# The second row's value sum over the experts: its last terms added by TensorE with the identity, in a new hand-written order of the whole program

## The chip, the cores and the metric

The kernel runs on one core of one Trainium2 chip. The metric is the device time of one execution in microseconds (us); the time of a kernel is the median of its runs. The granted TensorE clock of the profiled execution is 1.00.

## The reference, cut to what matters

The input x has two rows of 128 tokens and 512 channels, and a context of 2048 tokens stands beside each row. Three layers follow each other, each added to x: a perceiver layer (self-attention, cross-attention over the context, a feed-forward part, three layer norms), an RWKV7 layer whose scan runs over the two rows (so row 1 needs the state of row 0), and a SwitchHead attention over the 128 tokens of each row. The change is in the last one, with H = 8 heads of DH = 64, E = 5 experts and SEL = 2:

```python
q = (x @ Wq).reshape(b, t, h, dh).transpose(0, 2, 1, 3)
k = (x @ Wk).reshape(b, t, h, dh).transpose(0, 2, 1, 3)
gl_v = (x @ Ws).reshape(b, t, h, e)
wv = _topk_mask(gl_v, SEL) * jax.nn.sigmoid(gl_v)
xv = jnp.einsum('btd,edk->btek', x, Wv)
v = jnp.einsum('bthe,btek->bhtk', wv, xv)
scores = jnp.einsum('bhid,bhjd->bhij', q * scale, k)
probs = jax.nn.softmax(scores, axis=-1)
attn = jnp.einsum('bhij,bhjd->bihd', probs, v)
gl_o = (x @ Wd).reshape(b, t, h, e)
mask_o = _topk_mask(gl_o, SEL)
out = jnp.einsum('bthe,bthk,ekd->btd', mask_o, attn, Wo)
```

A head's value is the sum over the five experts of a gate times that expert's value. This sum, `v`, is what the change touches.

## The kernel before, in words

Tokens lie on the 128 partitions. Weights are multiplied in full f32 or, where they were split into a high and a low half (names with `hl_`), in fp32r. The phases are functions: queries, self-attention, cross-attention, feed-forward, `rwkv` and `switch_heads`, each called for row t = 0 and row t = 1. The weights of the later phases are loaded by SP's DMA queue while the earlier phases run.

**Order.** The phases do not run as they are written. `Program` records every engine call in a list, and `emit` issues the calls in the order of the list of numbers `ORDER` (lines 42 to 98), so that work of both rows and of several phases is interleaved by hand. Each engine runs its own instructions in that order and waits where an operand isn't ready. All recorded instructions have line 169 in the profile, the line in `emit`; they are told apart by the names of their tiles. DMA issues on SP are in the list too. Tiles come from pools that rotate: eight PSUM banks (`bank`), twenty row tiles (`row`), sixteen wide tiles (`wide`).

**switch_heads** (lines 1019 to 1150), for one row:

- `xn` is the normed row: its first half by DVE, its second by ACT, once a rinv has come from POOL. PE turns it (xnT).
- PE multiplies xnT with `fcat` (both gates' logits and the experts' values in one matrix of 400 columns, four matmuls), with `fWq` and with `fWk` (16 matmuls of 128x128 each). ACT copies gl, xv, qT and kT out of PSUM.
- DVE makes the gates: gt, eq, eq, gt and ahead count for each expert how many logits stand ahead of it, sel keeps those with fewer than two ahead, wv is the value gate.
- The value sum (lines 1058 to 1077): four products wv*xv go into the wide tile `ve`, the fifth into `v`, each 128x512; then three adds on DVE: `ve` 128x1024 (line 1075), `ve` 128x512 (line 1076), `v` 128x512 (line 1077).
- For each half of the heads PE makes the scores kT·qT, DVE reduces their negated maximum `nb`, ACT the exponentials `es`, PE turns them, ACT copies them (`eT`), and PE multiplies `v` with `eT` (v·eT).
- DVE spreads the result over the experts (`me`, two products of 128x1280 in row 0; one and three pieces in row 1) and adds the `me` parts. In row 0 PE turns the sum; in row 1 PE adds and turns it by matmuls with `unit`, an identity matrix in f32. ACT copies `aT`, PE multiplies with `fWo` (per row six matmuls of 128x256), DVE adds the residual (`res`), and SP stores it.

`keep_warm` (line 515) issues dummy matmuls of `unit` with `unit` into a bank that is overwritten later; TAILW holds their numbers in the tail. `matmuls` (line 344) accumulates a list of products in one bank, `project` (line 455) makes products in two halves of 256 columns, `Moments` (line 358) holds the steps of a norm.

In `rwkv`, what the prediction's steps touch stands at the end: `Y` is scaled by the gate `tg` and turned (yT), multiplied with `Wo` (eight matmuls of 128x256), the residual is added (`hh`), normed and turned (hhT), multiplied with `Wf` (eight matmuls); DVE adds the bias (`f`), ACT takes its tanh (`tf`), and after a norm the row `X` is updated, from which `switch_heads` takes `xn`.

Of the kernel before, what the change touches and what calls it, by code (L numbers as in the profile page):

```python
# [16 lines left out]
P = 128  # L17
# [5 lines left out]
HD = 64  # L23
H = C // HD
# [18 lines left out]
8 0 208 1708 1731 1 209+1 3 215+3 233 1732+1 219+2 211 4 2 232 234 21 235 212 236 213+1 20 25 222+3 228+1 237+4 244  # L43
248+1 270 245 242 22 230 271+1 246 23 273+2 247 26 24 276+1 27 278 231 250+9 279+4 260+5 284 266 285+4 267 37 28 31 34
19 38 226 29 292 30 243 318 32 293+1 33 319+2 295 227 35+1 322+4 39 296+5 43 46 44 47 327+2 302 290 48 40 303+2 269
306+2 330 41 268 309+5 45 11 5 42 9 315 331+6 291 338 317 414 339+2 358 344 359 415 316 69 84 70 49 375 343 345 376
342 50+1 416+1 377+1 360 346+1 12 379 57 418 380+1 18 419 348+2 361 351 382 58 423 79 383 420 13 16+1 15 421+1 14
384+2 352+2 74 355 387+2 424 59 362 390 425+2 363+2 356 391 357 392 428 366 395 367 429 393 368 6 60 87 369 430 394
1709 396+3 372+1 370 431 371 61 432 400 434 1710 402 401 1711 435 56 433 404 436 405 403 437+2 408+1 406 410 463 453
411 440 407 454 464 441 465+1 85 455 467 456 443 457 444 458 442 447 89 448 459 468 71 445 469 483 473 460 446 449 75  # L50
474 470 475 450 476 62 66 77 63 477 88 471 478+1 64 480 484+1 481 486+1 86 488 461 521 493+1 489+1 495 522 126 482 462
496+1 523+2 67 491 498+1 65 500 526 501 68 527+2 502 472 72 492 503+1 530+1 90 505+1 532 507+3 533 511+3 92 515+1 534
94 73 82 535+4 517 549 540 588 76 541+1 589 543 78 544 590 10 518 591+2 80 519 83 550+1 575 552 95 553 545 112 594 576
595 554 104 81 96 546 97 547 555 596 577 597 556 578 557+3 598 98 548 599 727 579+1 520 99 93 91 728 561 107+1 105 121
581+1 562 583 563+5 584 569+4 585 729 106 600 100 129 127 574 586+1 601+1 730+5 603+1 128 618 736 609+2 737+1 740 131
741+2 172 612 766 744+1 1734 767 753 101 746+1 754+1 748 756+1 102 758+1 749 607 605 608 768+5 606 613 137 122 103 760
614 761 623 615 142 641 624 774 625 750+1 642 130 626 109 643 762 644 775+1 374 123 763 173 152 124 616 627 764 777
113 125 628+8 645 739 646 136 659 637 660+1 638 662 639 134 765 114 778 132 617 752 640 647+4 663 145 110 53 664 779
652+1 780 133 781 111 782 654+3 789 783 796 785 135 787 658 55 665+2 677 668 678 669 786 619 784 788 143 679 670+1 790
680+1 672+4 682 138 140 683+2 791 620 792+1 801+2 819 804 820 115 621 174 622 794 837 821 838 686 688 822 839 687 840  # L60
689 147 805 54 807 692 795 146 141 139 693 808 806 809 797+1 116 810 690 811+1 696 813+1 697 815 823 144 824 816+2 694
691 148 698+3 118+1 702+1 855+1 117 704 695 120 705+2 841 149 842 857+1 150+1 52 412 160+1 413 708 710+1 709 712+2 187
171 859 188 825+11 843+3 715 178 153 451 847+7 189 179 860 720+1 716+1 861+2 722+1 718+1 864 904 916 905 866 180 867
865 906+1 917 908 868 874 162 875 909 876 870 877 871 724 928 198 725 869 163+1 799 878 918 910+1 154+1 872 879 157
165 452 156 170 158 175 873 913 880+3 800 884+1 726 159 912 914+1 919+2 886 922 888 176 923 887 925 929 889+1 924
930+1 891+1 932+1 193 934 177 197 926 935 927 936 194 937 893 938+1 184 940 894+1 898 896+1 899+2 957 969 958+1 970
941 943 196 942 944+2 951 948 947 960 952 949 953 950 954 961+1 185 955 963+1 971+2 966 974+1 965 967+1 956 976 978
977 169 195 982+3 1010 979 1012 1011 980 986 186 987+1 1013+1 168 989+2 1016 1015 1020 992+1 1017 1067 1028 1075 1089
1069 1090 1018 1093 1099+1 1107 1111 1022 1029 1092 1091 1101 1076 1102 1094 1142 1077 1030 190 902 1021 191 981 1071
1031 903 1068 1070 1078 1032 1095+1 1079 1108 1112 996 994 1026 1073 1110 1141 1024 997 995 192 998 1072 167 999  # L70
1080+2 1004 1001 1000 166 1083 1005 1002 1023 1084 1033 1006 1003 1103 1034 1109 1085 1007 1074 1008 1086 181 205 1139
182 1035+1 183 1009 1097 1219 1088 1221 1218 1220 1222 1025 1037+1 1224 1027 1039 1225 1223 1098 1113 1116+1 1019 1228
1323 1333 1324 1118 1114 1104 1226 1229 1305 1325 1327 1306 1119 1326 1328 1087 1045 1230+1 1105 1279 1281 1280 1282
1334+2 1329 1232 1344 1330 1233 1042 1283+1 1286+2 1234 1345 1041 1106 1115 1289 1285 1290 1235 1043 1291+2 1237 1046
207 1040 1238 1294 1239 1295 1240 1346 1047 1296 1236 1241 1297 1120 1044 1389 1331 1391 1332 1343 1352 1347 1307 1242
1353 199 1243 1143 1354+1 1244+1 1348 1246 1349+1 204 1140 1048 1054 1121 1337 1056 1065 1123 1122 1390 7 1338 1049
1124 1339 1125 1050 1059 1247 1052 1308 1135 1248 1309 1055 1392 1298+1 1127 1144 1310+2 1393 1061 1300 1058 1145
1340+1 1063 1053 1301 1356 1302 1316+1 1146 1342 1062 1064 1051 1060 1318 1148 1129 1133 1057 1351 1066 1126 1303 1253
203 1319 1376 1136 1252 1357 1249 1137 1251 1256 1304 1254 1250 1138 1255 1377 1130 1358 1257 1264 1258 1260 1378 1262
1131+1 1153 1313 1128 1154 1265 1359 1263 1261 1134 1320 1267 1149+2 1147 1394 1259 1395 1271 1155 1274 1152 1379 1156  # L80
1314 1321 1158+1 1315 1157 1371 1161 1360 1396 1160 1397 200 1170+1 1162 1322 1276 1398 1164 1380 1273 1373 1163 1165
1172+1 1272 1166+1 1277 1268 1374 1190 1361 1375 1278 1381 1270 1174 1383 1175 1168 1269 1367 1382 1362 1364 1169 1366
1384 1363 1176 1275 1177 1372 1385 206 1178 1386+2 1179+1 1368 1365 1369 1266 1370 1399+1 1198 1404 1406 1405 1407+1
201 1401+1 1181+2 1186 1184 1187 1191 1185 1192 1188 1193 1189 1194 1199+1 1195 1409 1403 1196 202 1410+1 1197 1201+4
1412 1415 1413+1 1424 1416+1 1425+1 1206+1 1212 1209 1208 1213 1210 1214 1211 1215+2 1473 1472 1427 1418+2 1475+1 1474
1477 1421 1428 1478 1422 1429 1423 1479+1 1487 1481 1488 1482 1430+3 1435 1483 1522 1489 1434 1436+2 1484 1523 1227
1485 1444 1440+1 1439 1450 1505 1442 1451+1 1443 1453 1506+3 1445+1 1486 1447 1496+1 1490+3 1454+1 1458 1524 1498+1
1513 1525 1500+1 1514+1 1502 1511 1516 1526 1517 1503 1518 1494 1510 1448 1512 1449 1459 1456+1 1460 1495 1519+2 1527
1461 1528 1466 1529 1504 1539 1530 1540+1 1463 1462 1467 1464 1468 1465 1469 1542 1470+1 1533 1604+1 1531 1606+1 1610
1608 1559 1609 1560+1 1532 1543 1562 1619 1544 1549 1611 1534 1545 1613 1550 1612 1614+2 1546 1552 1536 1547 1553 1563  # L90
1565 1564 1569 1620 1570 1566 1535 1617 1548 1643 1537 1551 1567 1538 1621+1 1555+1 1554 1638 1637 1639+2 1654 1642
1618 1571 1645 1557 1655 1646+1 1628+1 1558 1648+1 1572+2 1656 1650 1657 1651 1579 1652 1630+1 1575 1623 1632+1 1576+2
1634+1 1624+2 1658 1653 1659 1627 1636 1660+2 1698+3 1671 1568 1644 1664 1667 1665+1 1663 1672+2 1681 1715 1682+1 1716
1582 1580 1583 1581 1587 1688+2 1717 1684 1584 1702+1 1705 1585 1675 1679 1676 1685 1718 1677+1 1712 1691 1588 1692
1686 1589 1668 1706 1704 1586 1590+1 1713 1719 1669 1687 1670 1694 1693 1695+2 1592 1714 1721 1707 1727 1680 1720
1725+1 1722+2 1593 1599+2 1594 1728 1735 1729 1741 1730 1747 1595 1736+1 1596 1738+1 1742+3 1748+2 1740 1751 1597+1
1746 1758 1752 1759 1602 1760+2 1753+2 1603 1756+1
"""
OPT = set("""psc me2 z1d fc2 Wv Wk u2col bfpe z4pe z1pe q2 hhcol q2row d3 both1 both4""".split())

ON_ACT = [set("vsum vc vv bv".split()), set("vsum vc vv bv".split())]
PCR = [{0,1,2},{0,1,2}]
WHOLE = set("Wv1 Wv2 fc2 Wv Wk".split())
VPE = set()
MIX = {"Wq1": 2}
MIXD = set("Ww Wa Wr".split())
Z4D, BFD = {0, 1}, {1}
CUTW = 2
HNORM = "dve"
ACC = set()  # L110
TAILW = (4, 4, 4, 3, 3)
WIDE_W = set("Wq1 Wk1".split())
NDUM, TDUM, HLB, WDB, UNS = 8, 0, 4, 8, 0


class Halves:

# [68 lines left out]
def perceiver_kernel(ctx: ExitStack, tc: tile.TileContext, a: dict, out: bass.AP):  # L186
# [832 lines left out]
    def switch_heads(t):  # L1019
# [91 lines left out]
        for par in range(2):  # L1111
# [11 lines left out]
            if not t:  # L1123
                dve.tensor_add(me[par][:, 0:2], me[par][:, 0:2], me[par][:, 2:4])
# [112 lines left out]
```

## Time and profile before

| what | value |
| --- | --- |
| runs of the kernel before | 221.88, 222.58, 222.99 us; median 222.58 us |
| the profiled execution | 221.38 us |
| its span, first to last instruction | 219.5 us |
| recorded instructions | 3664 |
| DMA | 43.42 MB, mean 198 GB/s |

The profiled execution's time stands 1.9 us above its span and 1.2 us below the median of the runs. Times in the profile count from the start of the span. A line of a timeline gives start, duration, engine, line, operation, output and inputs, shapes and the number of instructions merged in it; in square brackets stands the idle time of the engine before it and what released it. A plain f32 matmul leaves two records in the trace, a transpose or an fp32r matmul one. Recorded durations of neighbouring instructions overlap by a little, so that sums are made from start to start.

### The profile page before, as it was taken

Reading aid. Unit: us, or ns where it says so; the run is one execution under the profiler, and the core shown is the slowest. Engines: PE = TensorE matmul, PEld = TensorE weight load, DVE = VectorE, ACT = ScalarE, POOL = GpSimd, SP = SyncE. Lnnn points to the kernel's source line nnn. Section 1 sums busy time; section 2 is a strip of 40 time slices with the busy share of each in tenths; the row PEclk is TensorE's granted clock in tenths of the full one; section 3 lists DMA queues with packets and bytes.
Section 4 is the critical chain, followed back from the end, with each engine's and each line's share of the span. In section 5 each row is a group of like instructions: output and inputs, shape, how many; then the busy total and the mean of one; then the engine's idle time right before and its main releaser. Section 6 shows DMA issues by size and latency. Waiting matters only on the chain.

```text
span 219.5 us, 3664 instructions
## 1 busy us (share of the span) xinstructions
PE 211.3 (96%) x1228; PEld 178.2 (81%) x1228; DVE 190.0 (87%) x452; ACT 141.2 (64%) x400; POOL 17.6 (8%) x40
## 2 busy tenths in 40 slices
PE   6999999999999999999999999999988999999993
PEld 6999779988787758868788888887765799799892
DVE  4691688999999999988999999999997689999871
ACT  2766578873799899626579599988642524813710
POOL 4200020000000000010120200040302111000000
PEclk9999999999999999999999999999999999999999
DMA  5999999049699894887999999000000000000002
GB/s 181 349 384 378 382 389 361 26 134 362 253 358 392 318 325 157 276 311 263 298 378 401 344 387 355 35 1 0 3 0 0 0 3 1 0 3 0 0 25 73
DMA packets 21897, 43.42 MB, mean 198 GB/s; under 512 B 1283, under 2 KB 2871, under 8 KB 21879
## 3 DMA queue, kind: packets, MB, share of 16 engines
q1 hardware_dynamic: 21879, 43.19, 55.2%
q8 instruction: 10, 0.16, 0.3%
q14 instruction: 8, 0.07, 0.1%
HBM read 42.66 MB, written 0.52 MB: 197 GB/s over the span
## 4 chain that ended last, share of the span: by engine, by line
PE 58%; DVE 23%; issue 11%; POOL 3%; ACT 3%; POOLq 0%; DVEq 0%; ACTq 0%
PE bank L169 58%; DVE ve L169 3%; DVE Y L169 2%; DVE st L169 2%; POOL rinv L169 2%; DVE me L169 2%; DVE nb L169 1%; DVE X L169 1%; DVE v L169 1%; DVE f L169 1%; POOL rs L169 1%; DVE pr L169 1%; DVE gt L169 1%; DVE eq L169 1%; ACT es L169 1%
## 5 line engine op out<-in xcount | busy, mean ns | idle before, releaser
L169 POOL TENSOR_TENSOR rinv<-ve,nhalf 128x1 f32<-128x1 f32 x16 | 10.4, 651 | 146.9 <-DVE ve L169 137.0
L169 DVE TENSOR_TENSOR hl_ctxT<-cT,hl_ctxT 128x1024 fp32r<-128x1024 f32 x16 | 18.9, 1217 | 0.2 <-ACT hl_ctxT L169 0.2
L169 PE MATMUL bank<-hl_ctxT,qkTh 128*128 128x512 f32 x64 | 18.4, 400 | 0.0
L169 ACT CAST hl_ctxT<-cT 128x1024 fp32r<-128x1024 f32 x16 | 16.3, 1052 | 3.3 <-DMA cT<-in_ctxT_dram 3.3
L169 PE MATMUL bank<-hl_ctxN,pTh 128*128 128x512 f32 x48 | 16.2, 410 | 0.0
L169 DVE TENSOR_TENSOR hl_ctxN<-cN,hl_ctxN 128x1024 fp32r<-128x1024 f32 x12 | 14.3, 1215 | 0.0
L169 PEld LDWEIGHTS bank<-hl_ctxT,qkTh 128*128 128x128 f32 x64 | 11.8, 188 | 2.7 <-DVE some L169 0.3
L169 DVE TENSOR_TENSOR hl_Wv<-w_Wv,hl_Wv 128x512 fp32r<-128x512 f32 x12 | 8.0, 684 | 5.2 <-ACT hl_Wv L169 5.2
L169 ACT CAST hl_ctxN<-cN 128x1024 fp32r<-128x1024 f32 x12 | 12.3, 1050 | 0.0
L169 PE MATMUL bank<-unit 128*128 128x128 f32 x58 | 9.3, 315 | 1.7 <-POOL unit masks.py:199 1.7
L169 PEld LDWEIGHTS bank<-unit 128*128 128x128 f32 x58 | 8.8, 229 | 2.0 <-POOL unit masks.py:199 1.7
L169 PEld LDWEIGHTS bank<-hl_ctxN,pTh 128*128 128x128 f32 x48 | 8.9, 188 | 2.0 <-DVE pTl L169 0.2
L169 PE MATMUL bank<-xnT,w_fWq 128*128 128x128 f32 x64 | 10.0, 280 | 0.0
L169 PE MATMUL bank<-hl_ctxT,qkTl 128*128 128x512 f32 x32 | 9.8, 394 | 0.0
L169 PE MATMUL bank<-hl_ctxN,pTl 128*128 128x512 f32 x24 | 9.6, 400 | 0.0
L169 PE MATMUL bank<-xnT,w_fWk 128*128 128x128 f32 x64 | 9.4, 277 | 0.0
L169 PEld LDWEIGHTS bank<-xnT,w_fWq 128*128 128x128 f32 x64 | 8.6, 192 | 0.5
L169 PEld LDWEIGHTS bank<-u2T,w_fc 128*128 128x128 f32 x64 | 7.9, 191 | 1.3 <-ACT u2T L169 0.6
L169 PEld LDWEIGHTS bank<-xnT,w_fWk 128*128 128x128 f32 x64 | 8.3, 192 | 0.6
L169 ACT CAST hl_Wv<-w_Wv 128x512 fp32r<-128x512 f32 x12 | 7.4, 620 | 2.0 <-DMA w_Wv<-in_Wv_dram 1.9
L169 PE MATMUL bank<-u2T,w_fc 128*128 128x128 f32 x64 | 8.2, 277 | 0.3 <-ACT u2T L169 0.3
L169 PE MATMUL bank<-w_Wr,mix 128*128 128x256 f32 x32 | 8.5, 379 | 0.0
(291 smaller groups left out, 607.0 us busy)
## 6 DMA issues: line engine op xcount, KB each, us to landing
cT<-in_ctxT_dram SPq DMA_DIRECT2D x8, 1024.0 KB, 8.2
cN<-in_ctx_dram SPq DMA_DIRECT2D x8, 1024.0 KB, 6.7
spread<-in_spread_dram SPq DMA_DIRECT2D x9, 512.0 KB, 8.4
w_Wv<-in_Wv_dram SPq DMA_DIRECT2D x12, 256.0 KB, 5.4
w_Wk<-in_Wk_dram SPq DMA_DIRECT2D x8, 256.0 KB, 5.0
w_Wq<-in_Wq_dram SPq DMA_DIRECT2D x4, 256.0 KB, 3.7
w_Wk2T<-in_Wk2T_dram SPq DMA_DIRECT2D x4, 256.0 KB, 8.7
w_Wq<-in_Wq_dram SPq DMA_DIRECT2D x1, 1024.0 KB, 11.5
```

The costliest lines, as they stand in the source:

```text
L169: self.tc.keep_in_program_order(op(*args, **kwargs))
```

## The change

In row 1 (`VPH = {1}`), the adds of lines 1076 and 1077 are no longer made by DVE. A new PSUM bank `pv` takes three matmuls of PE with `unit`, moving `v`, `ve[:, 0]` and `ve[:, 1]`, each 128x512 f32, accumulated; a second row tile named `v` takes the result by an ACT copy of 128x512. The 1024-wide add of line 1075 stays on DVE, and so does the whole sum in row 0. The new constant HS0 is 0, with which the lines around `me` do what they did.

```diff
+VPH = {1}
...
+HS0 = 0
...
             dve.tensor_add(ve[:, 0:2, :], ve[:, 0:2, :], ve[:, 2:4, :])
-            dve.tensor_add(ve[:, 0, :], ve[:, 0, :], ve[:, 1, :])
-            dve.tensor_add(v, v, heads(ve[:, 0, :]))
+            if t in VPH:
+                pv = bank([P, H, HD])
+                matmuls(pv.rearrange("p h d -> p (h d)"), [(unit, x) for x in (v.rearrange("p h d -> p (h d)"), ve[:, 0, :], ve[:, 1, :])], True)
+                v = heads(row("v"))
+                act.copy(v, pv)
+            else:
+                dve.tensor_add(ve[:, 0, :], ve[:, 0, :], ve[:, 1, :])
+                dve.tensor_add(v, v, heads(ve[:, 0, :]))
...
-            if not t:
+            if not t and HS0 < 2:
                 dve.tensor_add(me[par][:, 0:2], me[par][:, 0:2], me[par][:, 2:4])
-        if t:
+        if t or HS0:
```

Apart from this, no instruction is added or taken out: PE has three matmuls more, DVE two operations fewer, ACT one more. The extra bank and the extra row tile shift the rotation of the later ones of row 1 by one place. The list `ORDER` is replaced as a whole. On the engines this moves, among others:

| engine | before | after |
| --- | --- | --- |
| SP | w_Ww, ..., fWo, w_Wg, fWk, fWq, w_Wo, w_Wf, fcat | fWk, w_Wo, fWq, w_Ww, w_Wg, w_Wf, fcat, fWo |
| DVE | xn of row 0, then the hh adds of row 1 | hh adds of row 1, then xn of row 0 |
| DVE | gate work of row 0 (gt to wv) and one ve product ahead of xn of row 1 | behind it |
| DVE | me of row 0, among it nb of row 1, then the 1024-wide add of row 1 | nb of row 1 twice and the 1024-wide add, then me of row 0 |
| PE | fcat of row 0 ahead of Wf of row 1 | behind it |
| PE | scores of row 0, first half, ahead of xn's transposes of row 1 | behind them |
| PE | v·eT of row 0 ahead of the scores of row 1 | seven of eight behind them |
| PE | thirteen dummies from 201 us on | nine there, four between Wf of row 0 and the fWk matmuls of row 0 |
| PE | the last fWo matmul of row 0 among the unit·me matmuls | behind them; one fWo matmul of row 1 among them |

## The prediction

> **What bounds the kernel now.** I read the page first (busy shares, slices, chain), then the chain in order of time, then a table of busy time by stage, then the timelines of VectorE (DVE), ScalarE (ACT) and TensorE (PE) from 160 us on. On the page:
>
> ```profile
> PE 211.3 (96%) x1228; PEld 178.2 (81%) x1228; DVE 190.0 (87%) x452; ACT 141.2 (64%) x400; POOL 17.6 (8%) x40
> ...
> DVE  4691688999999999988999999999997689999871
> ...
> DMA  5999999049699894887999999000000000000002
> ...
> PE 58%; DVE 23%; issue 11%; POOL 3%; ACT 3%; POOLq 0%; DVEq 0%; ACTq 0%
> ```
>
> PE is nearly full, DVE less so, and the transfers are over by slice 26 (143 us). The chain in order of time runs on PE to 116 us, on DVE from 146 to 168, on PE to 174, on DVE to 203, on PE to the end. The change sits in the last part, so the stages there decide (the columns are the stretch, its length, then busy time and instructions of PE, PE's weight loads, DVE, ACT, POOL):
>
> ```profile
> 162.00:168.80 6.80, 5.41 (x23) 3.44 (x21) 5.85 (x20) 1.15 (x3) 1.20 (x2) 1.00 0.00 0
> 168.80:184.00 15.20, 15.18 (x99) 13.04 (x100) 11.46 (x34) 6.07 (x17) 2.06 (x3) 1.00 0.01 2
> 184.00:201.00 17.00, 17.00 (x132) 15.08 (x132) 16.68 (x31) 7.98 (x31) 0.01 (x1) 1.00 0.00 1
> 201.00:207.20 6.20, 5.89 (x49) 5.22 (x48) 5.44 (x13) 4.22 (x20) 0.00 (x0) 1.00 0.00 0
> 207.20:219.50 12.30, 8.87 (x57) 7.81 (x55) 6.31 (x11) 1.28 (x4) 0.00 (x0) 1.00 0.13 44
> ```
>
> From 168.8 to 201 PE has no gap, and from 184 DVE has hardly one: two full engines, each of which could take the end. The two adds that go stand here on DVE:
>
> ```profile
> 204.09 0.48 DVE L169 TENSOR_TENSOR me<-me 128x320 f32<-128x320 f32 x1
> 204.49 0.69 DVE L169 TENSOR_TENSOR ve<-ve 128x512 f32<-128x512 f32 x1
> 205.21 0.69 DVE L169 TENSOR_TENSOR v<-v,ve 128x512 f32<-128x512 f32 x1
> 205.82 0.17 DVE L169 RECIPROCAL ri<-sm 128x4 f32<-128x4 f32 x1
> ...
> 207.16 1.49 DVE L169 TENSOR_TENSOR me<-bank,mo 128x1280 f32<-128x1280 f32 x1 [0.66 <-PE bank L169]
> ```
>
> They are on the path: PE's v·eT of row 1 waits for v, and DVE then waits 0.66 us for v·eT. From 204.49 to 205.82 the adds take 1.33 us start to start. If that were all, the gain would be 1.33 + 0.66 = 2.0 us. But the whole order is new, and its other moves count as much. Below, a duration is start to start where instructions follow each other without a gap (a DVE operation begins some 0.07 us before its predecessor's recorded end).
>
> **What replaces them.** No row shows a 128x512 sum with `unit`. Nearest is cN·pT, plain f32 with 512 columns, two records to a matmul:
>
> ```profile
> 78.94 3.60 PE L169 MATMUL bank<-cN,pT 128*128 128x512 f32 x8
> 82.37 0.82 PE L169 MATMUL bank<-ident,em 128*128 128x128 f32 x6
> ```
>
> Four matmuls in 82.37 - 78.94 = 3.43 us, 0.86 each: three cost 2.57 us. Below, 0.7 us (three at the 0.23 of an fp32r matmul of that width, zT·fc2); above, 3.6 us (six records at their mean of 592 ns). I take 2.57, the same form. ACT's copy from PSUM takes 580 ns (the pT copy, 128x512). In the new order DVE does both nb reduces and the 1024-wide add of row 1 before the me work of row 0, not after it. So v is under way on PE and ACT while DVE does me of row 0: after the add, scores' exps on ACT hold PE for about 0.3, then the three matmuls 2.6, transposes and dummies between them 0.6, the copy 0.8 with its waits, eT copy and v·eT 0.6: 4.9 us. DVE needs about 6.0 for me of row 0 and the small steps (below). The wait is covered with 1 us to spare, and just covered at 3.6. Behind the waiting v·eT on PE stand me's transposes of row 0 and its fWo; on ACT the eT copies stand behind v's copy, and they are in the 4.9.
>
> **What is moved, 162 to 184 us.** What stands ahead of what on each engine I read from the two programs' orders. Before 162 nearly the same sets of work stand ahead of each milestone. Then: (1) both halves of hh of row 1 are added before row 0's xn, because the eighth Wo matmul no longer stands behind xn's transposes. The second add comes at about 168.4 instead of 169.73, hh about 1.1 us earlier. (2) Row 0's four fcat matmuls (0.67 each, 170.16 to 173.74) go behind Wf of row 1, fWq and fWk matmuls and four dummies come forward. On PE, 12 matmuls at 0.224 and the transposes put Wf's end at about 176.9 instead of 177.7; f's second add on DVE comes 1.0 earlier. (3) DVE's gate work of row 0 leaves this stretch:
>
> ```profile
> 174.20 0.57 DVE L169 TENSOR_TENSOR gt<-gl 128x400 bf16<-128x400 f32 x1 [1.14 <-ACT gl L169]
> 174.69 0.57 DVE L169 TENSOR_TENSOR eq<-gl 128x400 bf16<-128x400 f32 x1
> ...
> 176.10 0.57 DVE L169 TENSOR_REDUCE ahead<-gt 128x80 f32<-128x400 bf16 x1
> 176.61 0.42 DVE L169 TENSOR_TENSOR f<-bank,spread 128x256 f32<-128x256 f32 x1
> ```
>
> It lay in waits for Wf: f's add at 176.61 follows Wf's first bank (matmuls to 176.4), not the gate. Taking it out gains nothing here; behind xn, where DVE is full, it costs 2.5 us, and a ve product (0.6) goes with it. With f's second add at 177.0 instead of 177.97 and the same steps after it, row 1's xn starts at about 183.1 instead of 184.12.
>
> **The sum, DVE.** From xn at 183.1 to the first nb of row 1: xn and its nb 0.4; gate and sel of row 0 2.5; two nb 1.2; wv 0.2; five products 3.0; the three adds of row 0 2.4; ri 0.1; gate, sel and wv of row 1 2.8; five products 3.0. Together 15.6: DVE is there at 198.7. **PE.** After Wf at 176.9 come 19 matmuls at 0.224 and four fcat at 0.67, 6.9 us: xn's transposes of row 1 at about 183.9. Before, transposes (185.00) to first kT·qT of row 1 (199.41) took 14.4 without a gap; now row 0's first four score matmuls come in (183.83 to 185.00: 1.2), seven of eight v·eT of row 0 go behind (0.2 each: 1.4). So 14.2: kT·qT at 198.1, its first bank (0.86) read from 199.2. PE is the later by half a microsecond, and PE sets the time. From 199.2 DVE does nb, ri and mo 0.75, nb 0.6, the 1024 add 1.15 (to 201.7), then mo 0.1, two me products 2.8, three 640-wide adds 2.2, ri twice 0.2, the 320-wide add 0.4, mo twice 0.3. Row 1's me starts at 207.7, before at 207.16: **+0.55**. After it, DVE's work is the same, but one fWo matmul of row 0 (0.43) now stands after the last me sum, where PE works without a gap to the end: **+0.43**. Sum +1.0: profiled execution 221.38 + 1.0 = 222.4. The median of the runs, 222.58, stands 1.2 above the profiled one; the median after is then 223.6 us (+0.45%).
>
> Costed at nothing: SP's reordering. Wg goes behind fWk, Wo, fWq and Ww. Its old landing is 116.5 + 8.6 = 125.1; in the new place about the same bytes stand ahead of it as ahead of the old Wo, which landed at 118.5 + 15.9 = 134.4; its first matmul is at 139.2. If that cover failed, every late microsecond would count whole. fWo, now last, has from 143 to 207. Dummies moved from 201 to 160-175 fill waits there; 0.22 each if they don't.
>
> **A rule weighed.** From 168.8 to 201 PE's matmul row is full. The Trainium skill, Perfetto Trace Analysis, section "Identifying the Most-Contended Engine", holds that this row is a poor measure and that weight-load busy time tells the headroom. By the table's weight loads, 15.08 of 17.00, PE would have 1.9 us of room from 184 to 201. By it the DVE sum (198.7) would stand alone and the total be +0.5 instead of +1.0. The trace speaks against it: fWq matmuls follow each other at 0.224 us throughout, and I take the row.
>
> **Rivals.** *A, the gain shows (0.15).* The adds and the stall go (-2.0), and the gate finds waits behind xn: 222.58 - 2.0 = 220.6. For it: these adds were on the path. Against: DVE has 0.3 us free from 184 to 201, and PE cannot have row 1's scores ready before 199. *B, earlier upstream (0.18).* PE idles 1.4 us and DVE 0.95 from 162 to 168.8, DVE 1.0 from 110 to 162; if the order wins 1.2 there, the time is 222.4. Against: DVE's work ahead of row 1's Y is the same set. *C, PE falls further behind (0.22).* Between xn and kT·qT of row 1 nothing is left to fill PE's waits: fWk stands straight behind xn's transposes, and row 0's es transposes need exps that come after a later gate. With no slack at 199.2, every wait there goes to the end, from the first. Two waits like those of 164.2 (0.63) and 168.8 (1.05) give +1.7 more: 225.3. Against: in the old order such waits were filled. *D, it does only what the sum says (0.45)*, 223.0 to 224.2.
>
> **The numbers.** About 0.5% (1.1 us) is what a measurement of this kernel can tell from no change. D gives 0.25 within it and 0.20 slower; A 0.15 faster; B 0.15 within and 0.03 faster; C 0.22 slower. Faster 0.18, same 0.40, slower 0.42. The range takes in D, B, most of C and a share of A: 221.2 to 225.4. D's own range is 223.0 to 224.2.
>
> **What would show it.** Right: two adds fewer at the end, three matmuls with `unit` of about 0.86 us each, no DVE wait for PE ahead of row 1's me; row 1's xn near 183.1, a DVE gap of about 0.5 us ahead of its first nb at 199.2, me at 207.7, last fWo 0.43 later after it. Wrong: xn later than 183.5 (step 1 or 2), nb at once after the products (PE was not the bound), a wait ahead of me (the cover fails), or milestones before 162 shifted by over 0.5 us, which I cost at nothing.

## The result, and the profile after

The changed kernel takes **224.08 us** (median of 21 runs, 222.38 to 225.38); the kernel before took 222.42 us beside it (21 runs, 221.47 to 223.24). The ratio is **1.0063, 95% interval 1.0045 to 1.0080**: slower by 0.6%. The profiled execution took 222.65 us with a span of 220.7 us, 1.27 and 1.2 us more than before.

Two lines of the page, the busy times and the shares of the chain of work that ended last:

```profile
PE 212.8 (96%) x1234; PEld 178.8 (81%) x1234; DVE 189.8 (86%) x450; ACT 140.8 (64%) x401; POOL 16.9 (8%) x40
...
PE 80%; DVE 14%; DMA 1%; POOL 1%; issue 1%; ACT 1%; SPq 0%; DVEq 0%; POOLq 0%
```

The totals say little: PE is busy 1.5 us longer (three matmuls of 0.86 make 2.6; what makes up the difference isn't shown), DVE 0.2 less. Nor does the chain name the bound: in order of time it runs on PE from 168.86 to 195.39 us and again from 200.33 to the end, but it counts PE's dummies as work, and from 182.86 to 207.90 DVE is as full as PE. The table by stage says more (stretch, length, busy time and instructions of PE, its weight loads, DVE, ACT, POOL):

```profile
168.80:184.00 15.20, 15.14 (x103) 13.37 (x103) 8.64 (x27) 5.67 (x16) 1.76 (x3) 1.00 0.01 2
184.00:201.00 17.00, 16.23 (x128) 14.34 (x129) 16.38 (x34) 8.92 (x39) 0.00 (x0) 1.00 0.00 1
201.00:207.20 6.20, 6.20 (x42) 4.72 (x40) 6.17 (x10) 3.50 (x15) 0.00 (x0) 1.00 0.00 0
207.20:220.70 13.50, 10.04 (x65) 8.59 (x63) 7.04 (x14) 1.28 (x4) 0.00 (x0) 1.00 0.12 40
```

DVE has 2.8 us less to do from 168.8 to 184 (the gate work that was moved out), where it had waits; from 201 to 207.2 it had 0.8 us to spare before and has none now, although two of its operations are gone. PE for its part has lost 0.77 us between 184 and 201. The timeline of DVE shows where the time is set; two lines of before stand ahead of it, then those of after:

```profile
168.35 0.41 DVE L169 TENSOR_SCALAR xn<-X,mv,rinv 128x256 f32<-128x256 f32 x1 [0.73 <-POOL rinv L169]
184.12 0.41 DVE L169 TENSOR_SCALAR xn<-X,mv,rinv 128x256 f32<-128x256 f32 x1
```

```profile
168.30 0.41 DVE L171 TENSOR_SCALAR xn<-X,mv,rinv 128x256 f32<-128x256 f32 x1
...
182.86 0.41 DVE L171 TENSOR_SCALAR xn<-X,mv,rinv 128x256 f32<-128x256 f32 x1 [0.73 <-POOL rinv L171]
...
183.25 0.57 DVE L171 TENSOR_TENSOR gt<-gl 128x400 bf16<-128x400 f32 x1
...
196.69 2.49 DVE L171 TENSOR_TENSOR ve<-wv,xv 128x512 f32<-128x512 f32 x4
199.10 0.68 DVE L171 TENSOR_REDUCE nb<-bank 128x4 f32<-128x512 f32 x1
...
200.60 1.22 DVE L171 TENSOR_TENSOR ve<-ve 128x1024 f32<-128x1024 f32 x1
...
207.13 0.49 DVE L171 TENSOR_TENSOR me<-me 128x320 f32<-128x320 f32 x1
207.54 0.26 DVE L171 SCALAR_TENSOR_TENSOR mo<-sel,ri 128x20 f32<-128x20 f32 x2
207.90 1.49 DVE L171 TENSOR_TENSOR me<-bank,mo 128x1280 f32<-128x1280 f32 x1
```

Between row 1's xn (182.86) and row 1's me (207.90) no line of DVE has a wait in brackets: none stands behind `nb` at 199.10 or behind `me` at 207.90, and the longest gap between two operations is 0.11 us. DVE's own work is the bound there. It begins 1.26 us earlier than before (184.12) and ends 0.74 later (207.16). The wait of 0.66 us ahead of me is gone, as is the work of the two adds, and 2.5 us of gate work and a product of row 0 have come in. The timeline of PE over the same stretch, with row 1's scores first:

```profile
197.04 1.71 PE L171 MATMUL bank<-kT,qT 64*128 64x128 f32 x16
198.68 0.88 PE L171 MATMUL bank<-v,eT 128*128 128x64 f32 x6
200.33 0.33 PE L171 MATMUL bank<-ident,es 128*128 128x128 f32 x1 [0.77 <-ACT es L171]
...
202.40 1.02 PE L171 MATMUL bank<-v,unit 128*128 128x512 f32 x2
...
203.59 1.88 PE L171 MATMUL bank<-ve,unit 128*128 128x512 f32 x4
205.31 0.27 PE L171 MATMUL bank<-ident,es 128*128 128x128 f32 x1
...
208.90 1.95 PE L171 MATMUL bank<-w_fWo,aT 128*128 128x256 f32 x8
```

The two matmuls of ve take 205.31 - 203.59 = 1.72 us, 0.86 each. The scores that start at 197.04 are done when DVE comes to them at 199.10, and PE then stands idle for 0.77 us until the first exponentials, which need DVE's maximum `nb`, are there. Row 0's fWo matmuls begin at 208.90 (before: 207.91), and from there PE is full to the end: the last `res` add starts 8.38 us later (8.19 before). The lines of before for this, then the last one of after:

```profile
207.91 2.38 PE L169 MATMUL bank<-w_fWo,aT 128*128 128x256 f32 x10
...
216.10 0.42 DVE L169 TENSOR_TENSOR res<-bank,X 128x256 f32<-128x256 f32 x1 [0.87 <-PE bank L169]
```

```profile
217.28 0.42 DVE L171 TENSOR_TENSOR res<-bank,X 128x256 f32<-128x256 f32 x1 [0.44 <-PE bank L171]
```

Where the 1.27 us of the profile came from: row 0's xn starts at 168.30 (before: 168.35), so all of it arises behind that line. From there to the end of the span it is 52.40 us, before 51.15. This distance hardly depends on how early row 0's xn comes (it is 52.40, 52.36 and 52.42 in the profiles of the changed kernel, e6 and e9, where xn comes at 168.30, 169.24 and 168.68), and it is used below to compare profiles.

### The profile page after: what moved, and what is told of

It is laid out like the page before. It is cut to its first block, busy times and chain, and to the rows that moved or that the text cites. A ratio compares the mean times of both kernels' runs of the same rounds, so it can differ in the third digit from the quotient of the medians.

```text
span 220.7 us, 3683 instructions
## 1 busy us (share of the span) xinstructions
PE 212.8 (96%) x1234; PEld 178.8 (81%) x1234; DVE 189.8 (86%) x450; ACT 140.8 (64%) x401; POOL 16.9 (8%) x40
## 4 chain that ended last, share of the span: by engine, by line
PE 80%; DVE 14%; DMA 1%; POOL 1%; issue 1%; ACT 1%; SPq 0%; DVEq 0%; POOLq 0%
PE bank L171 80%; DVE Y L171 2%; DVE pr L171 2%; DVE st L171 2%; DVE ve L171 1%; DMA X<-in_x_dram 1%; POOL rinv L171 1%; DVE hh L171 1%; DVE v L171 1%; DVE bv L171 1%; DVE mv L171 0%; DVE X L171 0%; DVE nb L171 0%; DVE f L171 0%; DVE wd L171 0%
## 5 line engine op out<-in xcount | busy, mean ns | idle before, releaser
L171 PE MATMUL bank<-unit 128*128 128x128 f32 x58 | 11.2, 328 | 1.7 <-POOL unit masks.py:199 1.7
L171 PEld LDWEIGHTS bank<-unit 128*128 128x128 f32 x58 | 9.8, 236 | 2.6 <-POOL unit masks.py:199 1.7
L171 PE MATMUL bank<-hl_ctxT,qkTl 128*128 128x512 f32 x32 | 10.6, 397 | 0.0
L171 PEld LDWEIGHTS bank<-xnT,w_fWk 128*128 128x128 f32 x64 | 9.1, 192 | 1.3
L171 PE MATMUL bank<-xnT,w_fWk 128*128 128x128 f32 x64 | 10.2, 276 | 0.0
L171 PE MATMUL bank<-w_Wa,mix 128*128 128x256 f32 x32 | 8.6, 381 | 0.0
```

The lines of the kernel that those rows point to most:

```text
L171: self.tc.keep_in_program_order(op(*args, **kwargs))
```

## The experiments

My theory at first: VectorE, not TensorE, bounds the stretch from row 1's xn to its me, because gate work was moved behind xn; the edit itself would do harm without the new order. The rival was the prediction's picture: TensorE is the later engine. Later a second question came up: why the median lies 1.66 us above that of before where the profile shows 1.27. In the table, the ratio is to runs of the kernel before that were timed beside that kernel (medians 222.21 to 222.48), and the last column counts the runs whose mean granted TensorE clock is 0.992 or less (of full speed).

| kernel | row 0's xn to the end | median, runs | ratio to before, 95% interval | runs with mean clock of 0.992 or less |
| --- | --- | --- | --- | --- |
| before | 51.15 | 222.42, 21 | 1 | 1 of 91 (all runs beside the experiments) |
| changed | 52.40 | 224.08, 21 | 1.0063 (1.0045 to 1.0080) | 6 of 21 |
| e1 | 54.47 | 225.24, 6 | 1.0134 (1.0111 to 1.0158) | 0 of 6 |
| e2 | 56.61 | 227.32, 6 | 1.0210 (1.0182 to 1.0237) | 6 of 6 |
| e3 | 51.66 | 222.81, 12 | 1.0022 (0.9999 to 1.0045) | 0 of 12 |
| e4 | 52.45 | 224.95, 6 | 1.0120 (1.0091 to 1.0148) | 1 of 6 |
| e5 | 53.77 | 223.99, 7 | 1.0068 (1.0044 to 1.0092) | 2 of 7 |
| e6 | 52.36 | 223.18, 12 | 1.0043 (1.0018 to 1.0068) | 1 of 12 |
| e7 | 52.14 | 222.64, 12 | 1.0016 (0.9996 to 1.0035) | 0 of 12 |
| e8 | 51.36 | 223.48, 11 | 1.0048 (1.0032 to 1.0064) | 2 of 11 |
| e9 | 52.42 | 223.10, 12 | 1.0035 (1.0015 to 1.0054) | 0 of 12 |
| e10 | 51.56 | 222.45, 12 | 0.9996 (0.9977 to 1.0015) | 0 of 12 |
| e11 | 51.83 | 223.03, 12 | 1.0013 (0.9988 to 1.0038) | 0 of 12 |
| e12 | 51.61 | 222.70, 12 | 0.9995 (0.9967 to 1.0024) | 0 of 12 |

### e1: the new sum in the old order

```diff
 ORDER: that of before, row 1's last two adds replaced in place
-DVE tensor_add ve, DVE tensor_add v
+PE matmul x3 (unit with v, ve0, ve1), ACT copy v
```

> The new sum in the old order: PE's three matmuls and ACT's copy stand where the two DVE adds stood, nothing else is moved. Theory (the sum pays only under cover of row 0's me): the matmuls come behind the es transposes that end at 205.9, take 2.6, the copy 0.7, and v·eT starts at about 209.3 instead of 206.05; row 1's me at about 210.4 instead of 207.16; +3.2 us against the kernel before, about 225.6. Rival (the edit is good by itself, the two adds and the wait go): -1 to -2 us, about 221.

Measured: 225.24 us, ratio 1.0134 (1.0111 to 1.0158), 3.0 more than the runs of before beside it (222.27). The theory holds. The timeline of DVE and that of PE in e1:

```profile
206.41 0.18 DVE L171 SCALAR_TENSOR_TENSOR mo<-sel,ri 128x20 f32<-128x20 f32 x1
211.04 2.09 DVE L171 TENSOR_TENSOR me<-bank,mo 128x1280 f32<-128x1280 f32 x2 [4.45 <-PE bank L171]
```

```profile
206.48 1.02 PE L171 MATMUL bank<-v,unit 128*128 128x512 f32 x2
207.34 1.88 PE L171 MATMUL bank<-ve,unit 128*128 128x512 f32 x4
209.90 1.10 PE L171 MATMUL bank<-v,eT 128*128 128x64 f32 x8 [0.68 <-ACT v L171]
```

DVE stands idle for 4.45 us until the sum has gone through PE (206.48 to 209.2), ACT (the copy) and v·eT. The sum by TensorE is much longer than the two adds that it replaces; what makes it cheap in the changed kernel is the new order, which lets DVE do row 0's me meanwhile.

### e2: the new order with the sum on VectorE

```diff
-VPH = {1}
+VPH = set()
```

> The new order with the old sum: two DVE adds right behind the 1024-wide add, no matmuls with unit for v, no copy. Theory (in the new order DVE is the bound from xn to row 1's me and the matmuls are covered): the adds push me back by their 1.3 us, from 207.9 to 209.2; +1.3 against the kernel after, +2.9 against the kernel before, about 225.3. Rival (PE sets the time of the tail, so its 2.6 us count): about 1 us faster than the kernel after, near 223.

Measured: 227.32 us, ratio 1.0210 (1.0182 to 1.0237), 3.2 above the changed kernel, where 1.2 was expected. From row 1's first nb to its me it is 10.25 us, 1.45 more than in the changed kernel: that part is as expected. The rest is at PE; its timeline in e2, and the table of stretches (behind the busy time of POOL stands the granted clock):

```profile
210.51 0.90 PE L171 MATMUL bank<-ident,me 128*128 128x128 f32 x3 [3.41 <-DVE me L171]
...
212.81 3.73 PE L171 MATMUL bank<-w_fWo,aT 128*128 128x256 f32 x8
```

```profile
207.00:210.50 3.50, 0.10 (x1) 0.00 (x0) 3.47 (x9) 0.00 (x0) 0.00 (x0) 0.91 0.00 0
210.50:217.00 6.50, 6.49 (x24) 5.77 (x25) 5.40 (x10) 0.48 (x1) 0.00 (x0) 0.52 0.00 0
```

Without the three matmuls PE has nothing to do for 3.41 us, and for the 6.5 us behind that gap it is granted about half the clock (0.52): eight fWo records take 3.73 us, in the changed kernel 1.95. All six runs have a mean clock of 0.992 or less. From row 0's xn to the end e2's profile has 4.21 us more than the changed kernel's (56.61 to 52.40), of which 1.45 are the adds. I put the rest to the gap and the half clock behind it; no run has the adds without the gap.

### e3: row 0's gate back ahead of row 1's xn

```diff
 DVE
-xn (row 1), gt eq eq gt ahead sel wv, ve (row 0), nb (row 0)
+gt eq eq gt ahead sel wv, ve (row 0), xn (row 1), nb (row 0)
 PE
-Wf (row 1), fcat (row 0) among fWq and fWk
+fcat (row 0), Wf (row 1), fWq and fWk
```

> The kernel after, but row 0's gate (gt to wv) and one product of its sum stand ahead of row 1's xn again, in DVE's waits for Wf; for that the four fcat matmuls of row 0 change places with twelve fWq and fWk matmuls on PE, and the fcat load comes earlier. Theory (the gate work behind xn makes DVE late at row 1's nb): DVE is 3.4 us earlier there, PE's scores, ready at about 198.0, become the bound, nb starts at about 198.1 instead of 199.1, me at 206.9 instead of 207.9: -1.0 us against the kernel after, about 223.0. Rival (PE is the bound already, as the prediction had it): no change, 224.1.

Measured: 222.81 us, ratio 1.0022 (0.9999 to 1.0045), 1.27 below the changed kernel. The theory holds; in the profile the gain is 0.74 us (51.66 to 52.40), because part of what DVE saves becomes waits for PE. PE's own order is changed here too (the fcat matmuls), so the gain is that of both moves. DVE's timeline in e3:

```profile
184.99 0.41 DVE L171 TENSOR_SCALAR xn<-X,mv,rinv 128x256 f32<-128x256 f32 x1
...
187.26 1.29 DVE L171 TENSOR_REDUCE nb<-bank 128x4 f32<-128x512 f32 x2 [1.79 <-PE bank L171]
...
194.36 0.58 DVE L171 TENSOR_TENSOR eq<-gl 128x400 bf16<-128x400 f32 x1 [0.73 <-ACT gl L171]
```

This DVE timeline of e3 has two brackets where the changed kernel has none. The two engines are close together: with 3.4 us taken from the one, the other is the bound after 0.7.

### e4 and e8: one half old, one half new

e4 has the order of before up to the last add into row 1's Y, and the new order (with the new sum) behind it; e8 has the new order up to there, and the old order with the sum on VectorE behind it.

```diff
 ORDER
-all new
+e4: old up to Y (row 1), then new;  e8: new up to Y (row 1), then old
```

> Everything up to the last add into row 1's Y (161.5 us) in the old order, with the old order of the transfers, the rest in the new one. Theory (the loss is made behind 162 us): as the kernel after, +1.2 to +1.6 us, 223.6 to 224.1. Rival (the new order of transfers and of the first 162 us carries a part): no more than 223.2.

> The new order up to the last add into row 1's Y, and from there the order of the kernel before, with its sum on VectorE. Theory (of the 1.66 us, the profiles show 1.25 behind row 0's normalisation, so 0.4 is the front's): 222.6 to 223.0. Rival (the whole loss is the tail's, and the front is even or a gain): 221.9 to 222.4. The cut itself can cost some tenths, as it did in the other half (1.3 us there), seen as waits of VectorE between 163 and 172 us; those are taken off before the theories are compared.

Measured: e4 224.95 us, e8 223.48, both above what theory and rival said. At the place where the two orders are joined new waits came in, so neither settles what the front (everything ahead of row 0's xn) costs. In e4's DVE timeline a new wait of 1.20 stands ahead of an f step:

```profile
165.07 0.42 DVE L171 SCALAR_TENSOR_TENSOR f<-tf,bank 128x256 f32<-128x256 f32 x1 [1.20 <-ACT tf L171]
```

Its last part, 52.45 from xn to the end, is that of the changed kernel (52.40): the loss of the tail is there without the new front. In e8 there is a gap of PE of 1.26 us and one of 0.47 behind it, followed by half a clock (a line of PE's timeline, then the table of stretches):

```profile
164.68 0.77 PE L169 MATMUL bank<-ident,Y 128*128 128x128 f32 x3 [1.26 <-DVE Y L169]
```

```profile
163.00:165.90 2.90, 1.18 (x5) 0.35 (x4) 2.00 (x6) 0.77 (x2) 0.00 (x0) 0.98 0.00 0
165.90:169.40 3.50, 3.48 (x9) 2.61 (x10) 3.23 (x11) 0.38 (x1) 0.65 (x1) 0.53 0.00 0
```

Its tail (51.36) is near that of before (51.15), as the old tail should be. Its 1.1 us above before (223.48 to 222.40) hold these gaps and whatever the front costs.

### e5 and e12: w_Wa behind the w_Wv pieces

In the profiles with the new order ScalarE waited 1.4 to 3.1 us for a piece of w_Wv at 105 us, with the old order 0.3 to 0.8. In the new order the 1 MB of w_Wa is issued ahead of it.

```diff
 SP
-w_Wa, w_Wv, w_Wk, w_Wv, w_Wr
+w_Wv, w_Wk, w_Wv, w_Wa, w_Wr
```

> The changed kernel with one transfer moved on SP: the 1 MB w_Wa is issued behind the two w_Wv pieces that it stood ahead of (as in the kernel before, where it was issued at 103.94 us, behind the w_Wv piece of 102.32). First use of w_Wa is at 117.2. Theory (SP's reordering costs about half a us of the median: ScalarE's cast of w_Wv waited 1.4 us for its piece in the changed kernel's profile, and 3.1 in the two other profiles with the new order, against 0.3 to 0.8 with the old order; TensorE stood about 0.9 us later behind the long waits): the wait is below 1 us, and the median falls from 224.08 by 0.4 to 0.9, to 223.2 to 223.7. Rival (those long waits were chance of the memory, or are made up for before row 0's last normalisation): no change, 223.9 to 224.3.

> The kernel with all five terms of row 1's sum on TensorE (222.45 us), with w_Wa issued behind the two w_Wv pieces as in the experiment that moved it alone. In the profiles with w_Wa ahead, the w_Wv piece landed 2.9, 3.9, 4.1, 4.2, 4.6, 4.6 and 4.6 us behind its issue; with w_Wa behind or in the old order 2.7, 2.9, 3.2, 3.2, 3.3 and 4.3. Theory (w_Wa ahead costs the front about 0.5 on the average): 221.8 to 222.1, which would be 0.2 to 0.3% below the kernel before. Rival (what the piece's later landing costs is made up for before row 0's normalisation, as the unchanged median of 223.99 with w_Wa moved alone suggests): 222.3 to 222.7, level with the kernel before.

Measured: e5 223.99 us (the changed kernel: 224.08), e12 222.70 (without this move: 222.45). The medians are the rival's: the move changes nothing that these runs can tell. But it did not do what the theory asked of it either: the waits in the two profiles were 1.65 and 1.41 us, not below 1, and in e7 and e11, which have the same move, 1.19 and 2.79. With w_Wa ahead they are 1.37 (the changed kernel) to 3.11 (e2).

What these waits go with can be read from the profiles. In the changed kernel, e2, e6, e9 and e10, which have the same order up to row 0's xn, the wait is 1.37, 3.11, 3.09, 2.38 and 2.69 us, and that xn starts at 168.30, 169.69, 169.24, 168.68 and 169.34. So a long wait goes with a late start of the stretch of the change. With one and the same order the front differs by over 1 us between these five profiles, where the tails of three of them (the changed kernel, e6, e9) differ by hundredths. With the old front there are two such profiles, before and e1: 0.63 and 0.79 us, xn at 168.35 and 168.93.

The profile of e5 shows something else. Here are two stretches of e5, then the same two of the changed kernel:

```profile
199.70:201.20 1.50, 0.74 (x7) 0.74 (x7) 1.47 (x5) 1.25 (x7) 0.00 (x0) 1.00 0.00 0
201.20:204.80 3.60, 3.60 (x15) 2.95 (x15) 3.60 (x5) 2.30 (x12) 0.00 (x0) 0.54 0.00 0
```

```profile
199.60:201.10 1.50, 0.77 (x7) 0.77 (x8) 1.47 (x5) 1.28 (x7) 0.00 (x0) 1.00 0.00 0
201.10:204.70 3.60, 3.60 (x21) 2.59 (x21) 3.60 (x5) 2.16 (x12) 0.00 (x0) 1.00 0.00 0
```

The gap of PE is the same, 0.77 us by its timeline; in e5's profiled execution the clock is 0.54 for the next 3.6 us, and the mean clock of that run is 0.992. Then DVE waits 1.44 us for PE ahead of row 1's me. Six of the changed kernel's 21 runs have such a mean clock, with a median of 224.40; the ten with a full clock (0.999 or more) have 223.69, and spread from 222.38 to 224.81.

### e6: row 0's late fWo matmul moved back

```diff
 PE
-fWo (row 0, bank_614), unit·me x8, fWo (row 0, bank_614)
+fWo (row 0, bank_614) x2, unit·me x8
```

> The changed kernel with one instruction moved on TensorE: the third fWo matmul of row 0's second half (bank_614) goes back ahead of the sums of row 1's last experts, next to the second one. Theory of the prediction (that matmul stands behind the last me sum, +0.43): the end comes 0.43 earlier, median 223.6 to 223.7. Rival, from both profiles (TensorE's busy time is the whole of every stretch from 204 us to the end but the last, so a matmul moved back only pushes what stands behind it): no change, 223.9 to 224.3, and the last six fWo matmuls start at the same distance from row 1's first me product, 6.6 us.

Measured: 223.18 us, ratio 1.0043 (1.0018 to 1.0068). The median is lower than either theory said, but the profile speaks for the rival: from xn to the end 52.36 (52.40), from row 1's me to the last res add 9.30 us (9.38). PE's timeline in e6 is as full as before the move:

```profile
209.83 1.95 PE L171 MATMUL bank<-w_fWo,aT 128*128 128x256 f32 x8
211.70 1.16 PE L171 MATMUL bank<-unit,me 128*128 128x128 f32 x8
212.69 1.03 PE L171 MATMUL bank<-w_fWo,aT 128*128 128x256 f32 x4
213.56 1.28 PE L171 MATMUL bank<-unit,me 128*128 128x128 f32 x10
```

The matmul that changed places on the full engine did not change its end. This kernel's runs show how far a median can stray where the tail moves by 0.04: 0.9 us below the changed kernel, with intervals that overlap.

### e9: the gap filled

```diff
 PE
-v·eT x3, es transpose (row 1, waits 0.77), ..., dummy x3
+v·eT x3, dummy x3, es transpose (row 1)
```

> The changed kernel with three filler matmuls (unit with unit, 0.22 us each) moved from behind two of row 1's transposes to ahead of the first, into the 0.77 us in which TensorE waits for ScalarE's first exponential of row 1 (199.56 to 200.33 us in the changed kernel's profile). Theory (in some executions the granted clock drops to half for about 3.5 us behind that gap, as from 201.3 to 204.9 in the profile of the run with w_Wa moved, and with it the mean clock falls to 0.992 or less: 6 of 21 executions of the changed kernel, none of 41 of the kernel before): the gap is 0.1 to 0.2, at most 1 of 12 executions shows a clock of 0.992 or less, and the median falls by 0.2 to 0.5 to 223.6 to 223.9. Rival (the drop has another cause, or another gap makes it): the same share of low clocks, 2 to 5 of 12, and 224.0 or more.

Measured: 223.10 us, ratio 1.0035 (1.0015 to 1.0054), no run of 12 with a clock of 0.992 or less. The gap is gone from PE's timeline in e9:

```profile
199.06 0.88 PE L171 MATMUL bank<-v,eT 128*128 128x64 f32 x6
199.77 0.89 PE L171 MATMUL bank<-unit 128*128 128x128 f32 x6
200.71 0.33 PE L171 MATMUL bank<-ident,es 128*128 128x128 f32 x1
```

Taken together: of the kernels with the gap of 0.77 us at 200 (changed, e4, e5, e6; e2 has it too, beside its longer one) 10 of 46 runs have the low clock; of those without it behind the same part of the program (e3, e7, e9 to e12) 0 of 72. So the low clocks go with the gap. e9 alone says this less firmly than the whole: at a share of 10 in 46, twelve runs without a low clock would come by chance about once in twenty times, and the other kernels without the gap differ in more than the gap. The gain of the median, 0.98, is more than the 0.4 that the change of the clock explains (224.08 to 223.69), and the profile's tail is unchanged (52.42). The rest, like that of e6, is not explained. It isn't a shift of whole series, since e5 and e6 were timed in one and differ by 0.8, and the runs of before beside the series have medians of 222.27, 222.40, 222.48 and 222.21. The front, which differs by over 1 us between profiles, is where I would look.

### e7: more of row 0 ahead of row 1, with w_Wa moved

```diff
 DVE
-nb (row 0, waits 1.79), wv·xv
+wv·xv x2, nb (row 0)
 PE
-fcat (row 1) x3, fWk ..., fcat (row 1)
+fcat (row 1) x4, fWk ...
 SP
-w_Wa, w_Wv, w_Wk, w_Wv
+w_Wv, w_Wk, w_Wv, w_Wa
```

> The kernel with row 0's gate ahead of row 1's normalisation (222.81 us) with three more moves: w_Wa behind the w_Wv pieces; two more of row 0's ve products ahead of row 0's first maximum, where VectorE waited 1.79 us for TensorE; and row 1's last fcat matmul next to the third, because VectorE waited 0.73 us for its logits. Theory (VectorE's own work sets the end from row 1's normalisation on, and the front loses half a us to w_Wa): about 0.6 less between xn and row 1's first maximum (15.5 down to 14.9) and 0.4 to 0.9 in front: 221.3 to 221.9, below the kernel before. Rival (TensorE is now the bound there, its last score matmul ends at 200.5 in that profile whatever VectorE does, and the front's loss is chance): VectorE's waits only move to row 1's first maximum, 222.5 to 223.0.

Measured: 222.64 us, ratio 1.0016 (0.9996 to 1.0035). The median is the rival's. DVE's wait of 1.79 us is down to 0.55, but the next one has grown from 0.73 to 2.45; it stands ahead of row 1's logits, not ahead of row 1's first maximum, where the rival had it:

```profile
184.88 1.29 DVE L171 TENSOR_REDUCE nb<-bank 128x4 f32<-128x512 f32 x2 [0.55 <-PE bank L171]
192.49 0.57 DVE L171 TENSOR_TENSOR eq<-gl 128x400 bf16<-128x400 f32 x1 [2.45 <-ACT gl L171]
```

### e10 and e11: all five terms on TensorE

```diff
-dve.tensor_add(ve[:, 0:2, :], ve[:, 0:2, :], ve[:, 2:4, :])
 if t in VPH:
-    ... [(unit, x) for x in (v, ve[:, 0, :], ve[:, 1, :])]
+    ... [(unit, x) for x in (v, *(ve[:, e, :] for e in range(4)))]
-TAILW = (4, 4, 4, 3, 3)
+TAILW = (4, 4, 4, 0, 0)
```

> The changed kernel with row 1's whole sum on TensorE: all five terms through the unit matrix, so that VectorE's add of 1024 elements goes as well (1.22 us), and without the nine filler matmuls of the tail (9 by 0.22 = 2.0 us, against 2 by 0.86 = 1.7 more of the sum); row 0's v by eT matmuls stand together ahead of row 1's transposes, and the first term of the sum in TensorE's 0.77 us gap. Theory (from row 1's normalisation to its first me product VectorE is the bound, not TensorE as the prediction had it): row 1's me product comes 7.5 us behind its first maximum instead of 8.8, and the median falls by 0.8 to 1.3, to 222.8 to 223.3. Rival of the prediction (TensorE sets the time there): VectorE waits for TensorE by what it saved, 223.8 to 224.6.

> The same five terms on TensorE in the kernel with row 0's gate ahead of row 1's normalisation and w_Wa behind the w_Wv pieces (222.64 us). If the two gains add, as they do where VectorE's work is the bound throughout: 0.8 to 1.2 less, 221.4 to 221.8, 0.3 to 0.4% below the kernel before. Rival (the gate's move has already brought VectorE to TensorE's pace, as its waits of 0.6 and 2.5 us for TensorE's banks and logits suggest): 222.3 to 222.8, VectorE waiting for a bank ahead of row 1's me product.

Measured: e10 222.45 us, ratio 0.9996 (0.9977 to 1.0015), 1.6 below the changed kernel and level with before; e11 223.03, ratio 1.0013 (0.9988 to 1.0038). In e10 row 1's me comes 7.96 us behind its first nb, not 8.80, so DVE's add was on the path; the theory said 7.5. The median is below the theory's range (222.8 to 223.3), and the add is not alone in it: PE has 0.3 us less to do here, its gap of 0.77 is filled, and no run has a low clock. What is left of the 1.22 us becomes a wait for PE, here in e10 and then in e11:

```profile
200.13 0.68 DVE L171 TENSOR_REDUCE nb<-bank 128x4 f32<-128x512 f32 x1
...
208.09 1.49 DVE L171 TENSOR_TENSOR me<-bank,mo 128x1280 f32<-128x1280 f32 x1 [0.39 <-PE bank L171]
```

```profile
207.93 1.49 DVE L170 TENSOR_TENSOR me<-bank,mo 128x1280 f32<-128x1280 f32 x1 [0.81 <-PE bank L170]
```

With both gains in one kernel (e11) the wait grows to 0.81 us: they do not add up, as its rival said, though the median is above the rival's range (222.3 to 222.8) too. Five orders of this work (e3, e7, e10, e11, e12) end within their uncertainty of the kernel before, and none clearly below it.

## Why the prediction was right or wrong

The forecast of +1.0 us for the profiled execution and 223.6 for the median stood against +1.27 and 224.08. The sign, the stage and the cause in general (the gain of the adds is spent on work moved behind xn) were right. That the sum came so near is partly luck, since one milestone was right for the wrong engine and one term for the wrong reason. Point by point:

- **Row 1's xn at 183.1: right** (182.86). hh came earlier and Wf ended sooner, as read from the orders.
- **TensorE is the later engine at row 1's first nb (199.2 against DVE's 198.7): wrong.** This is the step that failed, and the prediction's own sign of it came: nb stands straight behind the products, without the gap of 0.5 us. PE's scores start at 197.04 instead of 198.1, so that their first bank is ready at about 198.0, and DVE comes at 199.10. On PE, row 1's transposes began 0.3 earlier than worked out, and row 0's eight score matmuls, which the profile of before puts at 1.17 and 1.09 for the two halves, took 1.64 together (183.92 to 185.56). On DVE the work from xn to nb was 16.24 us, not 15.6: the adds of row 0 took 2.6 for 2.4, the gate of row 1 3.1 for 2.8. PE was about 1.1 earlier than worked out and DVE 0.4 later, so that the time (199.1 for 199.2) came out right for the wrong engine, which is luck. That DVE is the later one is read from the timelines of after: DVE has no wait there, and PE stands idle for 0.77 us behind the scores. e3 and e10, whose moves touch PE as well, agree: with less work on DVE the end comes 0.7 to 0.9 us earlier, and then DVE waits for PE.
- **The rule on weight loads**, which the prediction set aside in favour of the matmul row (the Trainium skill, Perfetto Trace Analysis, "Identifying the Most-Contended Engine"), came nearer for this step: PE did have room, and DVE was the bound. But the 1.9 us of room read from it were not there either; 0.77 us of idle PE is what the trace of after shows from 184 to 201.
- **Row 1's me at 207.7 (+0.55): nearly right**, 207.90 (+0.74). No wait for PE stands ahead of it; the cover of the sum held, with 0.5 us to spare rather than 1: from the end of the 1024-wide add (201.73) to the end of v·eT's first four (about 207.4) it is 5.7 us, not 4.9.
- **Three matmuls with `unit` at 0.86: right.**
- **One fWo matmul behind the last me sum, +0.43: right in size, wrong in cause.** From me to the last res add it was 9.38 us, before 8.94: +0.44. But e6, with that matmul back in place, has 9.30. PE is full from row 0's fWo to the end in both kernels, so what counts is when row 0's fWo can begin: 207.91 before, 208.90 after. By the timelines that is because row 0's me now stands behind row 1's nb on DVE and ends at 207.62 instead of 204.57, with PE's transposes of it at 207.68; no run moves it alone. It gives 0.25 of the 0.44 (fWo begins 0.99 later, me 0.74); the other 0.19, by which the stretch from fWo on is longer, isn't explained. The prediction priced the place of one instruction, and should have followed row 0's me.
- **SP's reordering at nothing: open.** In the profile of after row 0's xn is where it was (168.30), but the w_Wv piece's wait is longer in the new order and in other profiles goes with an xn up to 1.4 us later. Moving w_Wa showed no gain (e5, e12), nor did it take the wait away.
- **The gain of the two adds, 2.0 us "if that were all": not there by itself.** e1 and e2 show that the sum on TensorE costs 3.0 us in the old order, and the new order without it 5.0, a part of which is the half clock. Each needs the other, as the prediction's cover for the sum implies for the first.
- **Not foreseen: the gap of 0.77 us on PE and its clock.** Of the 1.66 us between the medians the profile has 1.25 behind row 0's xn; runs with a low clock lift the median by about 0.4 (224.08 against 223.69 for runs at full clock). The two add up, but that is an account that fits, not one that is shown: e6 and e9, with the same tail, have medians only 0.6 to 0.8 us above before.
- **The rivals.** A (the gain shows) fell: gate work found no waits behind xn. B (earlier upstream) fell: xn of row 0 is where it was. C had the right place, but the waits of PE that it priced did not come; the time there is DVE's work. (Its two example waits are 0.47 and 0.88 us in the brackets of the timeline of before, not 0.63 and 1.05.)

What stays open: whether the front of the new order costs some tenths (e4 and e8 have waits of their own where the orders are joined, and two profiles with the old front are too few), and why the medians of e6 and e9 lie 0.5 us below that of the changed kernel's full-clock runs with the same tail.

## What to carry to other kernels

Where two engines are both nearly full, do not ask which is the bound but by how much the other one is behind: here 0.7 to 0.9 us, and what was saved on DVE beyond that turned into waits for PE (e3, e10). A sum moved to TensorE was longer here than the adds it replaced (2.6 us and a copy of 0.6, for 1.33); it pays only if other work of VectorE lies beside it, and that work must be looked at itself, because what stands behind it (here row 0's output projection) becomes late. Look at gaps of PE in the tail not only for their length but for the clock behind them, and look at the mean clock of every run, since a profiled execution may have missed the drop.

## What the runs showed of the hardware

Three gaps of PE were followed by about half the granted clock: 3.41 us idle (e2), then 0.52 for 6.5 us; 1.26 us and, shortly after, 0.47 (e8), then 0.53 for 3.5 us; 0.77 us (e5), then 0.54 for 3.6 us. The shortest did it only in some runs: by the mean clocks in 10 of 46. An idle time of 1.0 us between 167 and 171 us, ahead of the transposes of row 0's xn, which the profiles of e3, e7 and e9 to e12 all have (1.00 to 1.01), left no low clock in their 72 runs; so length alone does not decide, and what does is open.

The Trainium skill, TensorE: Matmul & The Clock Gate, section "Part 1: The HAM clock gate", says that half rate returns after an idle window of about 3.4 us. e2's gap of 3.41 us is of that length, though its clock was down before the gap ended (0.91 over the 3.5 us from 207.00); e5 and e8 do not agree with it, for their gaps were 0.77 us, and 1.26 with 0.47 behind it.
